# Two steps trade places in layer 3 of a four-layer transformer: keys and queries with a projection, a rotation with an addition

## The chip, the cores and the metric

The kernel runs on one core of one Trainium2 chip. The metric is the time of the whole program on the device in microseconds. The core's engines work side by side, each through its own list of instructions in order: TensorE (PE in the profile, its weight loads PEld), VectorE (DVE), ScalarE (ACT), GpSimd (POOL) and SyncE (SP), which issues transfers alone. GpSimd can issue transfers too, out of the same list as its arithmetic. The transfers of both run on the core's 16 DMA engines.

## What is computed

The input x has 4 batches of 1024 rows of 256 numbers, all in fp32. Four layers follow each other, each with a residual:

```python
x = x + attn_a(layernorm(x))     # layer 1: 16 heads of 64, no rotation
x = x + ffn(layernorm(x))        # layer 2: 256 -> 1024, gelu, -> 256
x = x + attn_b(layernorm(x))     # layer 3
x = x + ffn(layernorm(x))        # layer 4, the same weights as layer 2
```

Layer 3 normalises once more inside and adds that first normalised x as its residual. Its keys and queries come out of a narrow middle and are rotated by position:

```python
h = layernorm(x) * ln_scale + ln_bias
c_q, c_kv = h @ w_down_q.T, h @ w_down_kv.T            # 256 -> 128 each
q, k, v = (c @ up.T per head for the three w_up)       # 16 heads of 64
q, k = rope(q), rope(k)      # rows e, o -> e cos - o sin, e sin + o cos
out = softmax(q k^T / 8) v,  heads side by side,  @ w_out.T + x
```

## The kernel before

**Tiling.** A core's memory has 128 partitions, so two heads of 64 are worked on together, a *pair of heads*; there are 4 x 8 = 32 of them in an attention layer. For each, the 1024 queries are taken in 8 *steps* of 128. One step makes two score tiles of 128 x 1024 (`scores`, L238), their negated maxima on DVE (L249) and exponentials on ScalarE (L251), and one transposition in blocks of 32 on DVE (`turn`, L271, tile T). The blocks are then in the wrong partitions, and transfers bring them into the tile pT: of 15 for every two steps SyncE issues ten and GpSimd five (`send`, L295); in layer 3 one more is copied by ScalarE (`keep`, L287). Four to five steps later `weigh` (L304) multiplies pT by the values, `take` copies the sums (ScalarE, L314) and GpSimd divides them by the softmax's total (L316, tile oT, reading the totals out of pT). T and pT have two buffers each. The score tiles have three PSUM buffers, everything else that TensorE makes shares two (`group`).

**Projection.** `project` (L318 to L328) multiplies oT by the pair's rows of the output weights (L167 with `wo,oT`), ScalarE copies the product out of PSUM (`got`, L326), and GpSimd adds it to x (L328).

**Keys and queries.** While the steps of one pair of heads run, those of the next are made, in four turns, for two halves of the keys and two of the queries. `qk` multiplies (L167 with `hc,w`, four instructions) and copies to SBUF with a scale (L647). One step later `change` has GpSimd issue two transfers which bring each row to its neighbour's place (`turned`, L652, one buffer). One step after that `rotate` has GpSimd multiply by the cosines (L657, in place, so it too waits until the transfers have read the rows), multiply the turned rows by the sines (L658), and add (L659). `values` makes the values (L176, copied by L668) in two of the four turns.

**What sets the order.** The order is written out by hand in `steps_with` (L330 to L361): each engine does its part in the order in which the calls stand there. Odd jobs are put into `pieces` under the number of their step; a number lower by EARLY (0.5) puts them between the step's two halves of exponentials, a whole number at its end. With s the step:

- Even s: the scores of s+1; the five sends of GpSimd; `project`; the first exponentials of s+1; the pieces of s - 0.5, with `qk` and `values`; the second exponentials; the transposition of s; the pieces of s, with `rotate`.
- Odd s: the scores of s+1; the first exponentials; `weigh`; the second exponentials; `take`; the transposition; `keep`; the ten sends of SyncE; the pieces of s, with `change`.

The weights of a pair of heads are loaded by SyncE out of the same list as its sends (L636 and L212 to L214).

Of the kernel before, what the change touches and what calls it, by code (L numbers as in the profile page):

```python
# [9 lines left out]
F32 = mybir.dt.float32  # L10
# [5 lines left out]
P = 128  # L16
B, S, D = 4, 1024, 256
# [10 lines left out]
HB = 2  # L28
# [5 lines left out]
NK2 = S // DH  # L34
EPS = 1e-5
EARLY = 0.5


@with_exitstack
def hybrid_block_kernel(  # L40
# [5 lines left out]
    nc = tc.nc  # L46
# [18 lines left out]
    pp, tp, ptp, otp, tmp = pool("p", 2), pool("T", 2), pool("pT", 2), pool("oT", 1), pool("tmp", 1)  # L65
# [112 lines left out]
                    start=(i == 0), stop=(i == len(parts) - 1),  # L178
                )

    def attention(prep_batch, prep_pair, wo, loader, lead, kept):

# [18 lines left out]
        steps = [(g, qs) for g in range(len(pairs)) for qs in range(NT)]  # L203
        n = len(steps)
# [39 lines left out]
        def exponentials(s, j):  # L244
            if j == 0:
                probs[s] = pp.tile([P, NK, NG, SQ], F32, tag="p", name="p")
                total[s] = small.tile([P, 2], F32, tag="total", name="total")
            nmax = small.tile([P, 1], F32, tag="nmax", name="nmax")
            nc.vector.tensor_reduce(nmax, sc[s, j], AX.X, ALU.max, negate=True)  # L249
            place = j ^ (s % HB)  # L250
            nc.scalar.activation(  # L251
                probs[s][:, :NK2, ts(j, 2), :],
                sc.pop((s, j)).rearrange("p (k c i) -> p k c i", c=2, i=SQ), AF.Exp,
                bias=nmax, accum_out=total[s][:, place : place + 1],
            )
# [62 lines left out]
        def project(h):  # L318
            g, t0 = divmod(HB * h, NT)
            b, pr = pairs[g]  # L320
            po = group(HB, D)
            for t in range(HB):
                paired(po[:, t, :], [(oT[h][:, t], [wos[g][:, t]] * 2)])
            oT.pop(h)
            got = tmp.tile([P, HB, D], F32, tag="tmp", name="got")
            nc.scalar.copy(got, po)  # L326
            xd = xs[b][:, t0 : t0 + HB, :]
            nc.gpsimd.tensor_add(xd, xd, got)  # L328

        def steps_with(others):  # L330
            for k, f in others:
                pieces.setdefault(k, []).append(f)
            for s in range(-1, n + LAG + 1):
                h, part = divmod(s - LAG, HB)
                ahead = 0 <= s + 1 < n
                if 0 <= s < n:
                    invert(s)
                if ahead:
                    scores(s + 1)
                if part == 1 and 0 <= s // HB - 1 < n // HB:  # L340
                    send(s // HB - 1, nc.gpsimd, sent[len(sent) - POOL_DMA :])
                if part == 1 and 0 <= h < n // HB:
                    project(h)
                if ahead:
                    exponentials(s + 1, 0)
                for f in pieces.get(s - EARLY, ()):
                    f()
                if part == 0 and 0 <= h < n // HB:
                    weigh(h)
                if ahead:  # L350
                    exponentials(s + 1, 1)
                if part == 0 and 0 <= h < n // HB:
                    take(h)
                if 0 <= s < n:
                    turn(s)
                if part == 0 and 0 <= s // HB - 1 < n // HB:
                    keep(s // HB - 1)
                    T.pop(s // HB - 1)
                if part == 0 and 0 <= s < n:
                    send(s // HB, nc.sync, sent[: len(sent) - POOL_DMA])  # L360
                for f in pieces.get(s, ()):  # L361
                    f()

        return first, steps_with

# [126 lines left out]
    def layer_a():  # L492

        scale_a = 1.0 / (DH * DH * H)
        hTs = {}
        rows = Rows("a", (blocks[:1], blocks[1:2], blocks[2:]))

        def batch_a(b):
            work = []
            for qb in range(NQB):  # L500
                k = {}

                def straight(t, b=b, k=k, qb=qb):
                    if t == 0:
                        k["xn"] = xnp.tile([P, TQ, D], F32, tag="xn", name="xn")
                    dst, src = k["xn"][:, t, :], xs[b][:, qb * TQ + t, :]
                    shift, rstd = rows.factors(NQB * b + qb, t)[:2]
                    if b == 0 and qb == 1:
                        nc.vector.tensor_scalar(dst, src, rstd, shift, op0=ALU.mult, op1=ALU.add)
                    else:  # L510
                        standardize(dst, src, shift, rstd)

                def turned(c, b=b, k=k, qb=qb):
                    if c == 0:
                        p, tag = ((lowp, "low"), (highp, f"high{b % 2}"))[qb]
                        hTs[b, qb] = p.tile([P, NC, QB], F32, tag=tag, name="hT")
                    transposed(hTs[b, qb], k["xn"], c)

                work += [(10 * qb + t, lambda t=t, f=straight: f(t)) for t in range(TQ)]
                work += [(10 * qb + 6 + 2 * c, lambda c=c, f=turned: f(c)) for c in range(NC)]  # L520
            return work

        def pair_a(b, pr):
            made = {}

            def load():
                w = made["w"] = wp.tile([P, 3, NC, P], F32, tag="w", name="w")
                for i in (1, 0, 2):
                    nc.gpsimd.dma_start(
                        w[:, i], wqkv_a[i, :, ts(pr, P)].rearrange("(c p) f -> p c f", p=P)  # L530
                    )

            def qk(i, qb):
                name = ("qT", "kT")[i]
                if qb == 0:
                    made[name] = qkp.tile([P, S], F32, tag=name, name=name)
                pq = group(QB)
                paired(pq, [
                    (made["w"][:, i, c, :], [hTs[b, qb][:, c, :]] * 2) for c in range(NC)
                ])  # L540
                dst = made[name][:, ts(qb, QB)]
                if i == 0:
                    nc.scalar.mul(dst, pq, scale_a)
                else:
                    nc.scalar.copy(dst, pq)

            def values(m):
                if m == 0:
                    made["v"] = vp.tile([P, NK2, DH], F32, tag="v", name="v")
                pv = group(4, DH)  # L550
                for t in range(4):
                    qb, tt = divmod(4 * m + t, QB // DH)
                    by_head(pv[:, t, :], [
                        (hTs[b, qb][:, c, ts(tt, DH)], made["w"][:, 2, c, :]) for c in range(NC)
                    ])
                nc.scalar.copy(made["v"][:, ts(m, 4), :], pv)

            work = [(4 - 4 * i + 2 * qb - EARLY, lambda i=i, qb=qb: qk(i, qb)) for i in (1, 0) for qb in range(NQB)]
            work += [(6 + 2 * m, lambda m=m: values(m)) for m in range(NT // 2)]
            return {name: lambda name=name: made[name] for name in ("qT", "kT", "v")}, load, work  # L560


        later = [(4 + i, lambda i=i: rows.measure(2 + i // TQ, i % TQ)) for i in range(6 * TQ)]
        later += [(4 + 6 * TQ, lambda: rows.finish[2]())]
        first, steps = attention(batch_a, pair_a, wo_a, nc.gpsimd, lead=3, kept=0)
        loads, xn, pair = first[:2], first[2:14], first[14:]

        def measured(qb):
            for t in range(TQ):
                rows.measure(qb, t)  # L570
            rows.finish[qb]()

        def ready():

            nc.scalar.activation(small.tile([P, 1], F32, tag="nmax", name="ready"), eps, AF.Exp)


        first = loads + [lambda: measured(0)] + xn[:4] + [lambda: measured(1), ready] + xn[4:6] + pair[:1]
        first += xn[6:] + pair[1:3]
        later += [((-1, 0, 0, 1, 1)[i], f) for i, f in enumerate(pair[3:])]  # L580
        return first, lambda others: steps(later + others)


    def layer_b(rows):
# [45 lines left out]
        def pair_b(b, pr):  # L630
# [40 lines left out]
            for i in (1, 0):  # L671
                for qb in range(NQB):
                    k = 2 - 4 * i + 2 * qb
                    work += [(k - EARLY, lambda i=i, qb=qb: qk(i, qb))]
                    work += [(k + 1, lambda i=i, qb=qb: change(i, qb))]
                    work += [(k + 2, lambda i=i, qb=qb: rotate(i, qb))]
            work += [(4 + 2 * qb - EARLY, lambda qb=qb: values(qb)) for qb in range(NQB)]
            return {name: lambda name=name: made[name] for name in ("qT", "kT", "v")}, load, work

        return attention(batch_b, pair_b, wo_b, nc.sync, lead=5, kept=1)  # L680


    n_steps = B * NF * NT
# [72 lines left out]
```

## Time and profile before

| what | us |
|---|---|
| median of 3 runs | 3288.75 (3285.65 to 3289.74) |
| the profiled execution | 3283.29 |
| its span, first to last instruction | 3281.4 |
| layer 3's steps | about 1700 to 3060 of the span |
| busy over the span: PE, DVE, ACT, POOL | 3201.6, 2531.3, 2109.0, 1958.4 |

A row of the timeline has the start within the span, the duration, the engine, the line in the kernel, the instruction, what it writes and reads, shapes, and how many alike were merged; in brackets stands the time for which the engine was idle before it, and what ended that. A busy PE is not a PE at its peak, as the ends of matmuls are modelled. A row of the waits has the engine and line that waited, what it waited for, the total, the number of times and the longest. A wait for several things is put down to the one that came last by the profile, which can be wrong. DMA engines are no engine of the page's first line; their mean busy share is given for windows.

### The profile page before, as it was taken

How to read it: one execution, taken by the hardware profiler on the slowest of the kernel's cores; microseconds unless marked ns; L12 is line 12 of the kernel's file. 1: busy time of each engine (PE TensorE's matmuls, PEld its weight loads, DVE VectorE, ACT ScalarE, POOL GpSimd, SP SyncE). 2: the span in 40 equal slices, each digit the busy share in tenths (PEclk: the TensorE clock that was granted, in tenths of full speed). 3: DMA queues.
4: the chain of work that ended last, by engine and by line, in shares of the span. 5: the costliest groups of instructions: out<-in, count | busy, mean ns of one | idle time of the engine just before them, and what ended most of it. 6: DMA issues, size and time to landing. Idle time of an engine off the chain costs nothing.

```text
span 3281.4 us, 126564 instructions
## 1 busy us (share of the span) xinstructions
PE 3201.6 (98%) x52736; PEld 2022.3 (62%) x52736; DVE 2531.3 (77%) x2386; ACT 2109.0 (64%) x4304; POOL 1958.4 (60%) x2738
## 2 busy tenths in 40 slices
PE   8999999999999999999999999999999999998999
PEld 4666666666666666666555556666656666665666
DVE  7988888888888888941049889998989999998100
ACT  5666666666666666642447777777778777777332
POOL 4544454545444445430159888998989999996110
PEclk9999999999999999999999999999999999999999
DMA  8888888888888888840029889998888899998100
GB/s 226 224 220 213 226 223 222 219 227 223 222 214 218 222 229 225 218 116 0 2 81 237 223 217 240 242 240 236 240 229 240 240 243 247 245 246 214 38 20 20
DMA packets 244697, 642.13 MB, mean 196 GB/s; under 512 B 74304, under 2 KB 102976, under 8 KB 244128
## 3 DMA queue, kind: packets, MB, share of 16 engines
q1 hardware_dynamic: 161104, 397.60, 47.6%
q0 software_dynamic: 83024, 236.44, 25.8%
q8 instruction: 419, 6.86, 0.9%
q14 instruction: 150, 1.23, 0.1%
HBM read 43.39 MB, written 4.19 MB: 15 GB/s over the span
## 4 chain that ended last, share of the span: by engine, by line
PE 78%; SPq 8%; DMA 5%; DVE 3%; ACT 3%; issue 3%; POOL 1%; DVEq 0%; POOLq 0%; ACTq 0%
PE sc L238 23%; PE mm L304 21%; PE mm L167 16%; SPq L295 7%; PE mm L421 7%; PE ph L410 7%; PE mm L176 5%; DMA pT<-T 4%; DVE T L271 1%; DVE nmax L249 1%; ACT p L251 1%; PE mm L153 1%; POOL oT L316 0%; ACT gT L414 0%; SPq L214 0%
## 5 line engine op out<-in xcount | busy, mean ns | idle before, releaser
L249 DVE TENSOR_REDUCE nmax<-sc 128x1 f32<-128x1024 f32 x1024 | 1204.5, 1218 | 226.7 <-PE sc L238 223.5
L251 ACT ACTIVATE p<-sc,nmax 128x1024 f32<-128x1024 f32 x1024 | 1145.3, 1119 | 324.0 <-DVE nmax L249 324.0
L271 DVE STREAM_TRANSPOSE T<-p 128x2176 f32<-128x2176 f32 x512 | 1247.1, 2436 | 41.0 <-DMA pT<-T 17.6
L238 PE MATMUL sc<-kT,qT 64*64 64x512 f32 x8192 | 1085.5, 599 | 16.0 <-ACT p L251 10.6
L304 PEld LDWEIGHTS mm<-pT,v 64*64 64x64 f32 x32768 | 950.3, 133 | 145.6 <-issue 103.4
L304 PE MATMUL mm<-pT,v 64*64 64x128 f32 x32768 | 984.5, 269 | 14.5 <-issue 13.5
L295 POOL DMA_DIRECT2D pT<-T x1280 | 629.6, 499 | 121.1 <-PE sc L238 56.2
L316 POOL TENSOR_TENSOR oT<-oT,pT 128x256 f32<-128x256 f32 x256 | 186.1, 727 | 718.7 <-ACT oT L314 636.3
L238 PEld LDWEIGHTS sc<-kT,qT 64*64 64x64 f32 x8192 | 333.1, 133 | 409.9 <-issue 277.1
L328 POOL TENSOR_TENSOR x<-x,got 128x512 f32<-128x512 f32 x256 | 330.9, 1293 | 27.8 <-ACT got L326 23.9
L326 ACT COPY got<-mm 128x512 f32<-128x512 f32 x256 | 150.0, 586 | 283.0 <-PE mm L167 282.9
L428 DVE TENSOR_TENSOR x<-x,mm 128x512 f32<-128x512 f32 x32 | 22.0, 687 | 367.2 <-PE mm L421 367.1
L167 PE MATMUL mm<-wo,oT 128*64 128x256 f32 x2048 | 278.4, 393 | 19.6 <-POOL oT L316 18.6
L167 PEld LDWEIGHTS mm<-wo,oT 128*64 128x64 f32 x2048 | 124.6, 136 | 266.4 <-POOL oT L316 217.4
L414 ACT ACTIVATE gT<-ph,b_sb 128x512 f32<-128x512 f32 x128 | 87.5, 686 | 301.9 <-PE ph L410 301.8
L260 ACT COPY p<-total 128x128 f32<-128x128 f32 x512 | 151.8, 296 | 195.4 <-DVE total L259 188.5
L167 PE MATMUL mm<-hT,w 128*64 128x512 f32 x1024 | 242.9, 596 | 1.0 <-ACT hT L156 1.0
L421 PE MATMUL mm<-w_sb,gT 128*128 128x256 f32 x1024 | 226.0, 381 | 6.6 <-ACT hT L156 6.6
L410 PE MATMUL ph<-hT,w_sb 128*128 128x512 f32 x512 | 230.2, 603 | 0.5 <-ACT hT L156 0.5
L421 PEld LDWEIGHTS mm<-w_sb,gT 128*128 128x128 f32 x1024 | 193.1, 190 | 39.4 <-ACT hT L156 9.4
L396 POOL TENSOR_TENSOR x<-x,b_sb 128x256 f32<-128x256 f32 x64 | 44.5, 728 | 275.6 <-ACT xn L147 275.6
L251 ACT ACTIVATION_READ_ACCUMULATOR p<-sc,nmax 128x1 f32 x1024 | 205.3, 200 | 0.0
(90 smaller groups left out, 2473.1 us busy)
## 6 DMA issues: line engine op xcount, KB each, us to landing
pT<-T SPq DMA_DIRECT2D x2688, 136.0 KB, 4.7
pT<-T POOLq DMA_DIRECT2D x1280, 136.0 KB, 4.7
turned<-kT POOLq DMA_DIRECT2D x128, 128.0 KB, 3.5
turned<-qT POOLq DMA_DIRECT2D x128, 128.0 KB, 3.3
w<-in_wqkv_a POOLq DMA_DIRECT2D x96, 128.0 KB, 6.1
wo<-in_wo_a POOLq DMA_DIRECT2D x32, 128.0 KB, 5.4
wo<-in_wo_a POOLq DMA_DIRECT2D x64, 64.0 KB, 5.5
wo<-in_wo_b SPq DMA_DIRECT2D x32, 128.0 KB, 3.6
```

The source lines that it names most:

```text
L167: nc.tensor.matmul(out[ts(j, DH)], lhsT[:, ts(j, DH)], rhs[j], start=(first and i == 0), stop=(last and i == len(parts) - 1),)
L176: nc.tensor.matmul(out[ts(j, DH)], lhsT, rhs[:, ts(j, DH)], start=(i == 0), stop=(i == len(parts) - 1),)
L238: nc.tensor.matmul(sc[s, j][ts(half, DH), ts(m, 512)], qT()[rows, ts(2 * qs + half, DH)], kT()[rows, ts(m, 512)], start=True, stop=True,)
L249: nc.vector.tensor_reduce(nmax, sc[s, j], AX.X, ALU.max, negate=True)
L251: nc.scalar.activation(probs[s][:, :NK2, ts(j, 2), :], sc.pop((s, j)).rearrange("p (k c i) -> p k c i", c=2, i=SQ), AF.Exp, bias=nmax, acc ...
L271: nc.vector.transpose(T[h][:, :, q, :, :].rearrange("p c k i -> p k c i"), probs.pop(s))
L295: engine.dma_start(pT[h][ts(c, SQ), a], T[h][ts(a, SQ), c])
L304: nc.tensor.matmul(av[h][q][ts(j ^ q, DH)], v[ts(j, DH), k, :], pT[h][ts(j, DH), :, q, k, :], start=(k == 0), stop=(k == NK2 - 1),)
L316: nc.gpsimd.tensor_mul(parts, parts, pT.pop(h)[:, :, :, NK2, :])
L328: nc.gpsimd.tensor_add(xd, xd, got)
L410: nc.tensor.matmul(ph, w1_sb[:, c, ts(f, P)], hT[n][:, c, :], start=(c == 0), stop=(c == NC - 1),)
L421: nc.tensor.matmul(po[n][:, t % 2, :], gT[n][:, f, ts(t, P)], w2_sb[:, f, :], start=(f == 0), stop=(f == NF - 1),)
```

## The change

In layer 3 alone, `qk` moves from the place of EARLY to a new, earlier one (FIRST, 0.75), which lies directly ahead of `project`. `project` no longer copies and adds; it returns `fetch`, which copies and returns the addition. With `late` the copy comes after the first exponentials, and the addition at the very end of the step, after `rotate`. Layer 1 is called with `late=False`, which keeps its order. `values` stays where it is. No instruction is added or taken away.

```diff
+FIRST = 0.75
...
         for t in range(HB):
             paired(po[:, t, :], [(oT[h][:, t], [wos[g][:, t]] * 2)])
         oT.pop(h)
-        got = tmp.tile([P, HB, D], F32, tag="tmp", name="got")
-        nc.scalar.copy(got, po)
+
+        def fetch():
+            got = tmp.tile([P, HB, D], F32, tag="tmp", name="got")
+            nc.scalar.copy(got, po)
+            return lambda: nc.gpsimd.tensor_add(xd, xd, got)
+
         xd = xs[b][:, t0 : t0 + HB, :]
-        nc.gpsimd.tensor_add(xd, xd, got)
+        return fetch
...
-                if part == 1 and 0 <= h < n // HB:
-                    project(h)
+                for f in pieces.get(s - FIRST, ()):
+                    f()
+                fetch = project(h) if part == 1 and 0 <= h < n // HB else None
+                if fetch and not late:
+                    fetch()()
                 if ahead:
                     exponentials(s + 1, 0)
+                add = fetch() if fetch and late else None
                 for f in pieces.get(s - EARLY, ()):
                     f()
...
                 for f in pieces.get(s, ()):
                     f()
+                if add:
+                    add()
...
-                    work += [(k - EARLY, lambda i=i, qb=qb: qk(i, qb))]
+                    work += [(k - FIRST, lambda i=i, qb=qb: qk(i, qb))]
```

More of the change, by code (lines that the diff above doesn't have):

```diff
@@ L179, in by_head, with attention @@
                 )
-    def attention(prep_batch, prep_pair, wo, loader, lead, kept):
+    def attention(prep_batch, prep_pair, wo, loader, lead, kept, late):
         pairs = [(b, pr) for b in range(B) for pr in range(NF)]
@@ L564, in layer_a @@
         later += [(4 + 6 * TQ, lambda: rows.finish[2]())]
-        first, steps = attention(batch_a, pair_a, wo_a, nc.gpsimd, lead=3, kept=0)
+        first, steps = attention(batch_a, pair_a, wo_a, nc.gpsimd, lead=3, kept=0, late=False)
         loads, xn, pair = first[:2], first[2:14], first[14:]
@@ L678, in pair_b @@
             return {name: lambda name=name: made[name] for name in ("qT", "kT", "v")}, load, work
-        return attention(batch_b, pair_b, wo_b, nc.sync, lead=5, kept=1)
+        return attention(batch_b, pair_b, wo_b, nc.sync, lead=5, kept=1, late=True)
     n_steps = B * NF * NT
```

## The prediction

> **What bounds the kernel now.** I read the page first, then the windows, then one pair of steps in the timeline, then the waits. The page's first part, and windows over nearly all of layer 3 and over eight of its pairs of steps:
>
> ```profile
> PE 3201.6 (98%) x52736; PEld 2022.3 (62%) x52736; DVE 2531.3 (77%) x2386; ACT 2109.0 (64%) x4304; POOL 1958.4 (60%) x2738
> ```
>
> ```profile
> 1800.00:3000.00 1200.00, 1167.19 (x21732) 738.69 (x21728) 1093.82 (x943) 919.48 (x1841) 1068.62 (x1387) 1.00 0.89 237
> 2654.00:2734.00 80.00, 80.00 (x1508) 50.67 (x1504) 75.80 (x65) 61.81 (x124) 74.25 (x96) 1.00 0.94 248
> ```
>
> After the sum the columns are PE, PEld, DVE, ACT and POOL busy, the granted clock, the DMA engines' share, GB/s. GpSimd's 60% over the span is 93% in the eight pairs (74.25 of 80), DVE 95%, the DMA engines 94%. No engine has a microsecond to give in ten. One pair, first its even step:
>
> ```profile
> 2411.87 0.73 POOL L316 TENSOR_TENSOR oT<-oT,pT 128x256 f32<-128x256 f32 x1
> 2412.55 1.14 POOL L652 DMA_DIRECT2D turned<-kT  x2
> 2412.78 1.08 PE L167 MATMUL mm<-wo,oT 128*64 128x256 f32 x8
> 2413.68 2.44 POOL L295 DMA_DIRECT2D pT<-T  x5
> 2413.69 1.03 PE L167 MATMUL mm<-hc,w 128*64 128x512 f32 x4
> 2413.96 0.59 ACT L326 COPY got<-mm 128x512 f32<-128x512 f32 x1 [0.66 <-PE mm L167]
> 2414.45 1.12 ACT L251 ACTIVATE p<-sc,nmax 128x1024 f32<-128x1024 f32 x1
> 2415.55 0.60 ACT L647 ACTIVATE kT<-mm 128x512 f32<-128x512 f32 x1
> 2415.71 0.21 PEld L238 LDWEIGHTS sc<-kT,qT 64*64 64x64 f32 x8 [0.87 <-ACT p L251]
> 2416.14 1.30 POOL L328 TENSOR_TENSOR x<-x,got 128x512 f32<-128x512 f32 x1
> 2417.38 1.28 POOL L657 TENSOR_TENSOR kT<-kT,cos_sb 128x512 f32<-128x512 f32 x1
> 2421.75 0.73 POOL L316 TENSOR_TENSOR oT<-oT,pT 128x256 f32<-128x256 f32 x1 [0.50 <-DMA pT<-T]
> ```
>
> The loop that sets an undisturbed pair's 10.01 us is to be seen here: the projection (L167 from oT) follows the scores, the copy `got` follows it, the first exponential follows `got`, and the next scores wait 0.87 for that exponential, which frees their PSUM. GpSimd runs beside it: one multiplication (L316), two transfers of the turned rows (L652), five sends (L295), the addition (L328), three operations of the rotation, and 0.50 of waiting.
>
> **The change, by parts.** (1) *Keys or queries ahead of the projection.* Four matmuls of 1.03 move ahead of eight of 1.08, and the copy of 0.60 (L647) takes the place of `got` (0.59) ahead of the first exponential. Where L316 is in time the exponential starts where it did: between 0.05 earlier and 0.01 later; I take 0. Where L316 is late, something is won:
>
> ```profile
> PE mm L167 <- POOL oT L316: 17.4, 22, 3.3
> SPq L295 <- POOL oT L316: 17.3, 15, 3.5
> POOL qT L657 <- DMA turned<-qT: 8.3, 10, 1.4
> POOL kT L657 <- DMA turned<-kT: 7.8, 11, 1.1
> ```
>
> (waits between 1800 and 3000; total us, times, longest.) Counting from the end of the scores, the projection stood 19.9 us in 29 of the 114 pairs that lie whole between 1790 and 2990. Keys fill at most 0.93 of each (1.03 less the overlap of two groups), so 13.9. Layer 3 has 124 such pairs (32 pairs of heads by four turns, less the first four), so times 124/114: **-15.1 us**.
>
> (2) *`got` after the first exponential.* It trades places with L647, at equal length, and stands before the second exponential. It costs nothing while the projection ends before the first exponential does, 1.6 us later than now. Without that cover DVE, which in the same timeline works 9.84 of the 10.01 (four maxima 4.72, two transpositions 4.88, two reciprocals 0.24), would be late by the excess over 0.17. Nothing else on ScalarE queues behind it, and its reader, the addition, now comes 4 us later anyway.
>
> (3) *The rotation ahead of the addition.* No work is added. But L657 must wait for the two L652 transfers, and the addition of 1.29 was what stood between the last send and L657. From issue to landing (the turned tile's own view):
>
> ```profile
> DMA to landing us min/median/max: 2.0/3.4/5.3
> ```
>
> The second transfer is issued 0.57 after the first, the five sends end 1.14 + 2.43 = 3.57 after the first, so at the median the later transfer lands 0.57 + 3.4 - 3.57 = 0.4 after the sends, at the longest 2.3. Taken pair by pair from the landings, the wait without the addition is 0.74 on average (quarters at 0.12, 0.63, 1.06), against 0.16 that is waited now: 0.59 more in each pair. The Trainium skill speaks against this order in DMA: Bandwidth & Descriptors, Rules for kernel authors: issue early, compute, and wait late. Its price, in Anatomy of one DMA (fixed 2.0 us plus the bytes at 436 GB/s), would give an estimated 2.3 for these 128 KB, which lands 0.7 before the sends end: no wait at all, and only part (1) left, -15. The row says 3.4, on engines that are 94% busy, and the row decides.
>
> What takes the 0.59: GpSimd idles 0.72 a pair before L316 now, more than enough on average, but in 57 of 114 pairs less than what is added. Without waits its cycle is 9.33 (9.73 in its fastest pairs, less 0.40 of waiting); with 0.74 it is 10.07, above the loop's 10.01. So lateness of L316 builds up over undisturbed stretches and is worked off in disturbed ones (the mean pair is 10.52).
>
> What is late next: L316, behind it the transfers and sends of its own queue, the projection, and SyncE's sends, which wait until L316 has read the old pT (the second line of the waits). The projection tolerates 0.93 of keys plus the 0.29 by which L316 now ends ahead of the scores: 1.2, and up to 0.6 more in pairs without values, where PE stands before the scores anyway. SyncE tolerates on average 1.45: 0.43 in which it is still issuing weights, and 1.02 between the last landing and the transposition that reuses the tile two pairs on; a quarter of the pairs tolerate under 0.77. I carried the lateness through the 114 pairs, each with its own landing and idle time, and let the loop lose what exceeds a tolerance: 43.7 us lost at a tolerance of zero, 30.4 at 0.6, 24.0 at 1.0, 20.0 at 1.5. I take 1.0 to 1.5, times 124/114: 21.8 to 26.2, **+24 us**.
>
> GpSimd's sends to pT are late too, by a microsecond or so; they land about 3 us before SyncE's last one, so they cost nothing; were that cover gone, the transposition would wait. kT and qT are ready earlier, and nobody waits for them. The weights of the earlier matmuls land some 10 us ahead of their first use. Layer 1 has the old order.
>
> **Sum.** -15 + 0 + 24 = +9. The profiled execution took 3283.3 (span 3281.4 and 1.9 around it), so 3292 for its like; the runs' median lies 5.5 higher, at 3288.75, so **3298 us**.
>
> **Rivals.** *Faster:* the transfers land sooner than now, since the queue they share with SyncE's sends stands otherwise, or the idle time before L316 swallows the wait. With waits half as long the same carrying gives -11.5 at tolerance 1.0, with none -13.9: -13 to -15 for the layer, 3275. It decides from an average wait below 0.6, where loss and gain are even. For it: idle exceeds added wait on average. Against: 57 pairs in which it doesn't. *No change:* gain and loss even out, 3289; for it speaks that `got` and the keys' copy are of one length, so the loop keeps its 10.01 either way. *Much slower:* SyncE has no tolerance. Its sends start with L316 late, the DMA engines stand idle and then lag, the transposition waits. That is the tolerance of zero: 43.7 x 1.09 - 15.1 = +33, 3321; for it speak the engines' 94%, and a longer landing works alike (waits 20% longer at tolerance 1.0: +26). Against: most pairs have SyncE's last landing 0.6 or more ahead.
>
> **How the numbers follow.** Runs of this kernel can tell about 0.2%, 6.6 us. Chances: slower by 9 (7 to 12) 0.40, faster 0.24, no change 0.20, much slower 0.16. The first case reaches down to the 6.6 bound; I leave it with slower, as landings under load rather grow. Faster 0.24, same 0.20, slower 0.56. The range goes from 3272, a little below the case without waits (a loop 0.05 shorter in the 57 pairs without values adds 3), to 3325, just above the case without tolerance. The likeliest case's own range is 3289 to 3310.
>
> **What would show it.** (1) right: no wait of PE L167 on L316 above a few us, `got` behind the exponential in the timeline. (2) right: the second exponential not waiting for `got`. (3) right: L657's waits for the turned transfers grow from 16 to some 85 us, L328 directly ahead of L316, the 0.72 before L316 nearly gone, SyncE's waits for L316 above 17. If L657 waits under 60 us in total, the faster rival has won; if DVE's transposition waits tens of us for its transfers, the much slower one. Wrong altogether would be a shift in the undisturbed pair's 10.01, which no step of mine moves.

## The result and the profile after

The changed kernel takes 3300.34 us in the median of 15 runs, the kernel before 3285.78 in 15; the ratio is 1.0039, with a 95% interval of 1.003 to 1.0049. That is 12.8 us of 3286 (the prediction said 9); the two medians lie 14.6 apart. The profiled execution took 3299.06, its span is 3297.2.

The same two windows over layer 3, with the sum and then PE, PEld, DVE, ACT and POOL busy, the clock, the DMA engines' share and GB/s:

```profile
1800.00:3000.00 1200.00, 1150.85 (x21392) 710.41 (x21381) 1077.38 (x931) 911.40 (x1818) 1052.26 (x1370) 0.99 0.88 234
2654.00:2734.00 80.00, 80.00 (x1506) 49.10 (x1502) 74.98 (x64) 61.34 (x124) 70.92 (x93) 1.00 0.92 244
```

In the same 1200 us every engine gets less done: DVE begins 931 instructions instead of 943. In the eight pairs GpSimd falls from 74.25 busy to 70.92, not for want of work. Rows from the timeline of two pairs after the change, others left out, show why (L317 is now the multiplication into oT, L663 the turned rows' transfers, L296 the sends, L668 the rotation's first operation, L329 `got`, L330 the addition):

```profile
2652.37 0.73 POOL L317 TENSOR_TENSOR oT<-oT,pT 128x256 f32<-128x256 f32 x1 [0.56 <-ACT oT L315]
2653.04 1.13 POOL L663 DMA_DIRECT2D turned<-qT  x2
2653.41 1.08 PE L168 MATMUL mm<-hc,w 128*64 128x512 f32 x4
2654.17 2.43 POOL L296 DMA_DIRECT2D pT<-T  x5
2654.32 1.03 PE L168 MATMUL mm<-wo,oT 128*64 128x256 f32 x8
2654.54 0.60 ACT L658 ACTIVATE qT<-mm 128x512 f32<-128x512 f32 x1 [0.88 <-PE mm L168]
2655.03 1.11 ACT L252 ACTIVATE p<-sc,nmax 128x1024 f32<-128x1024 f32 x1
2656.12 0.58 ACT L329 COPY got<-mm 128x512 f32<-128x512 f32 x1
2657.12 1.27 POOL L668 TENSOR_TENSOR qT<-qT,cos_sb 128x512 f32<-128x512 f32 x1 [0.52 <-DMA turned<-qT]
2660.93 1.29 POOL L330 TENSOR_TENSOR x<-x,got 128x512 f32<-128x512 f32 x1
2662.40 0.73 POOL L317 TENSOR_TENSOR oT<-oT,pT 128x256 f32<-128x256 f32 x1 [0.19 <-ACT oT L315]
...
2668.07 1.28 POOL L668 TENSOR_TENSOR qT<-qT,cos_sb 128x512 f32<-128x512 f32 x1 [1.43 <-DMA turned<-qT]
...
2673.29 0.73 POOL L317 TENSOR_TENSOR oT<-oT,pT 128x256 f32<-128x256 f32 x1
```

The wait for the turned rows, 0.52 and then 1.43, stands where the addition stood, and the idle time ahead of L317 shrinks from 0.56 to 0.19 to nothing. Keys and queries run ahead of the projection, `got` behind the exponential, with no wait of its own here. The waits of layer 3 (total us, times, longest), after the change, between 1800 and 3000:

```profile
PE mm L168 <- POOL oT L317: 28.8, 34, 2.2
POOL kT L668 <- DMA turned<-kT: 51.7, 48, 2.7
POOL qT L668 <- DMA turned<-qT: 41.5, 43, 2.3
DVE T L272 <- DMA pT<-T: 24.4, 21, 3.1
SPq L296 <- POOL oT L317: 38.8, 37, 3.4
```

The same for the transposition before the change:

```profile
DVE T L271 <- DMA pT<-T: 7.9, 11, 2.0
```

The turned rows' landing after the change:

```profile
DMA to landing us min/median/max: 1.9/3.4/5.6
```

The transfers land as they did (3.4 in the median); what changed is that somebody stands waiting: 93.2 us instead of 16.1. The waits of TensorE and SyncE for L317 went up behind that. So did those of DVE's transposition: 60 us in all instead of 20, of which 42 instead of 13 are put down to transfers and the rest mostly to ScalarE.

One measure recurs below. *GpSimd's cycle* is the time from one of its multiplications into oT to the next, less the idle time just ahead of the latter, in pairs of steps in which GpSimd has no odd job besides the operations named so far, in the median. It was 9.36 before and is 10.14 after, against 10.01 for an undisturbed pair before the change.

### The profile page after: what moved, and what is told of

It is laid out like the page before. It is cut to its first block, busy times and chain, and to the rows that moved or that the text cites. A ratio compares the mean times of both kernels' runs of the same rounds, so it can differ in the third digit from the quotient of the medians.

```text
span 3297.2 us, 126564 instructions
## 1 busy us (share of the span) xinstructions
PE 3200.7 (97%) x52736; PEld 2004.9 (61%) x52736; DVE 2529.9 (77%) x2386; ACT 2111.2 (64%) x4304; POOL 1953.7 (59%) x2738
## 4 chain that ended last, share of the span: by engine, by line
PE 66%; SPq 15%; DMA 8%; DVE 3%; issue 3%; POOL 3%; ACT 2%; DVEq 0%; POOLq 0%; ACTq 0%
PE sc L239 18%; PE mm L305 17%; SPq L296 14%; PE mm L168 13%; DMA pT<-T 7%; PE mm L432 7%; PE ph L421 7%; PE mm L177 4%; DVE T L272 1%; DVE nmax L250 1%; POOL oT L317 1%; POOL x L330 1%; ACT p L252 1%; SPq L215 1%; PE mm L154 0%
## 5 line engine op out<-in xcount | busy, mean ns | idle before, releaser
L239 PE MATMUL sc<-kT,qT 64*64 64x512 f32 x8192 | 1072.4, 600 | 18.7 <-ACT p L252 12.3
L296 POOL DMA_DIRECT2D pT<-T x1280 | 629.7, 499 | 117.3 <-PE sc L239 56.9
L317 POOL TENSOR_TENSOR oT<-oT,pT 128x256 f32<-128x256 f32 x256 | 185.8, 726 | 660.2 <-ACT oT L315 648.2
L239 PEld LDWEIGHTS sc<-kT,qT 64*64 64x64 f32 x8192 | 317.7, 133 | 379.8 <-issue 290.6
L330 POOL TENSOR_TENSOR x<-x,got 128x512 f32<-128x512 f32 x256 | 329.0, 1285 | 20.4 <-ACT got L329 18.4
L329 ACT COPY got<-mm 128x512 f32<-128x512 f32 x256 | 149.7, 585 | 171.2 <-PE mm L168 170.7
```

The source lines that it names most:

```text
L239: nc.tensor.matmul(sc[s, j][ts(half, DH), ts(m, 512)], qT()[rows, ts(2 * qs + half, DH)], kT()[rows, ts(m, 512)], start=True, stop=True,)
L296: engine.dma_start(pT[h][ts(c, SQ), a], T[h][ts(a, SQ), c])
L317: nc.gpsimd.tensor_mul(parts, parts, pT.pop(h)[:, :, :, NK2, :])
L330: return lambda: nc.gpsimd.tensor_add(xd, xd, got)
```

## The experiments

Each time is a median, each ratio is to the kernel before on the same chip, for which 3282.2 to 3285.8 were measured. A single execution can lie some 10 us off its kernel's median (the profiled one of the first experiment took 3284.3), so verdicts are taken from the ratios, and places from the traces.

**Keys ahead without the rotation ahead.**

```diff
+                if add:
+                    add()
                 for f in pieces.get(s, ()):
                     f()
-                if add:
-                    add()
```

> The changed kernel with the addition to x back ahead of the rotation; keys and queries stay ahead of the projection and the copy 'got' stays behind the first exponentials. Theory A (the rotation's new place is what costs, keys ahead of the projection gain): L657's successor waits for the turned transfers for about 17 us in layer 3 again, TensorE's wait for L316's successor stays small, time 3286 - 15 = 3271, ratio to before 0.9954, not above 0.998. Rival B (the keys ahead or the late 'got' cost): same or slower than before, 3286 to 3300.

Measured: 3276.28, ratio 0.9972 (0.9965 to 0.998), so 9.2 us faster. Its waits:

```profile
PE mm L168 <- POOL oT L317: 9.8, 8, 3.4
POOL kT L668 <- DMA turned<-kT: 9.2, 13, 1.5
POOL qT L668 <- DMA turned<-qT: 4.8, 6, 1.7
```

The first half of the change is a gain, smaller than the 15 expected; TensorE's wait for the multiplication went down from 17.4. The profiled execution is one of this kernel's slower ones, no faster than the one profiled before the change, so its waits show the places better than the sizes. The distance from here to the changed kernel is the price of the rotation's place: 1.0039 less 0.9972, 22 us (by the intervals, some 4 either way). This kernel beats both the one before and the changed one.

**The rotation ahead alone.**

```diff
                 fetch = project(h) if part == 1 and 0 <= h < n // HB else None
-                if fetch and not late:
-                    fetch()()
+                add = fetch() if fetch else None
+                if add and not late:
+                    add()
+                    add = None
...
-                add = fetch() if fetch and late else None
...
-                    work += [(k - FIRST, lambda i=i, qb=qb: qk(i, qb))]
+                    work += [(k - EARLY, lambda i=i, qb=qb: qk(i, qb))]
```

> The rotation ahead of the addition alone: keys and queries back behind the projection, 'got' copied directly after it, as before. Theory A: the lateness of GpSimd now meets a projection that has no keys in front of it and stands ahead of the first exponential, with 0.3 us of tolerance; carried through the pairs this loses 36 x 1.09 = 39 us: 3325, ratio 1.012, clearly slower than the changed kernel (1.0039). Rival B: as before or at most as the changed kernel, 3286 to 3300.

Measured: 3310.62, ratio 1.0076 (1.0064 to 1.0088): 25 us slower than before, and clearly slower than the changed kernel.

```profile
PE mm L168 <- POOL oT L317: 38.7, 42, 2.2
POOL kT L669 <- DMA turned<-kT: 54.5, 50, 2.9
POOL qT L669 <- DMA turned<-qT: 34.3, 37, 2.2
```

89 us of waiting for the turned rows, nearly as in the changed kernel, without keys ahead. So the loss belongs to the rotation. But 39 had been expected for a tolerance of 0.3, and the loss is 25 here against 22 with keys in front, the same within the intervals: the tolerance matters far less than the prediction's carrying of lateness from pair to pair had it.

**Where `got` stands.** As the first experiment, with the copy directly behind the projection:

```diff
                 fetch = project(h) if part == 1 and 0 <= h < n // HB else None
-                if fetch and not late:
-                    fetch()()
+                add = fetch() if fetch else None
+                if add and not late:
+                    add()
+                    add = None
                 if ahead:
                     exponentials(s + 1, 0)
-                add = fetch() if fetch and late else None
```

> As e1_keys, but 'got' is copied directly after the projection, ahead of the first exponential, so that both copies stand ahead of it. My account of the loop (projection or keys, copy, first exponential, scores of the next step): each undisturbed pair grows from 10.01 by some 0.55, 124 x 0.55 = 68 us over e1_keys: about 3340, ratio 1.016. Rival (TensorE, VectorE or the DMA engines set the pair's 10.01 and ScalarE's order does not matter): within 10 us of e1_keys.

Measured: 3346.02, ratio 1.0181 (1.0168 to 1.0194), 69.7 over the first experiment, where 68 were expected. The timeline of ScalarE:

```profile
2660.06 0.60 ACT L659 ACTIVATE kT<-mm 128x512 f32<-128x512 f32 x1 [0.88 <-PE mm L168]
2660.98 0.58 ACT L329 COPY got<-mm 128x512 f32<-128x512 f32 x1 [0.32 <-PE mm L168]
2661.46 1.12 ACT L252 ACTIVATE p<-sc,nmax 128x1024 f32<-128x1024 f32 x1
```

The first exponential stands behind both copies and the end of the projection. The loop runs where the prediction put it: the order on ScalarE alone, with no work added, lengthens every undisturbed pair. The agreement of the sums is partly luck: undisturbed pairs went from 9.95 to 10.87, by 0.92 and not 0.55 (0.32 of waiting comes on top of the copy), but disturbed pairs hide much of it, and the mean pair grew from 10.50 to 11.02.

**The rotation a pair of steps later**, to take the landing away without moving the addition:

```diff
-    lowp, highp, xnp, rp = pool("low", 2), pool("high", 1), pool("xn", 1), pool("rope", 1)
+    lowp, highp, xnp, rp = pool("low", 2), pool("high", 1), pool("xn", 1), pool("rope", 2)
...
-                    work += [(k + 2, lambda i=i, qb=qb: rotate(i, qb))]
+                    work += [(k + 4, lambda i=i, qb=qb: rotate(i, qb))]
...
-    b2_sb = const.tile([P, D], F32, name="b2_sb")
+    b2_sb = w2_sb[:, 0, :]
...
-        nc.gpsimd.dma_start(b2_sb, b2.partition_broadcast(P))
```

> The changed kernel, but each rotation comes one pair of steps later, with two buffers for the turned rows, so that the transfers have some 10 us more to land; to make room b2 is not loaded and a row of w2 is added in its place. Theory A: the rotation's waits for turned vanish (below 5 us), what part (1) gains is left: 3271 or a little less, ratio 0.995. Rival (it is the addition's place behind the rotation, not the landing, that costs): stays at 3300, ratio 1.004.

Measured: 3456.18, ratio 1.0518. A miss by another cause, as the waits show:

```profile
PE sc L238 <- POOL qT L669: 128.6, 27, 6.6
```

(Between 1800 and 3100.) The waits for the turned rows are gone, but a pair of steps later is too late for the first half of the queries. Its rotation (under step 6 of the pair before, where it was 4) now stands at the end of the last even step before the next pair of heads starts, and GpSimd finishes it some 4 us after TensorE could have made that pair's first scores, which read it:

```profile
2014.81 1.26 POOL L669 TENSOR_TENSOR qT<-qT,turned 128x512 f32<-128x512 f32 x1
2016.12 3.57 PE L238 MATMUL sc<-kT,qT 64*64 64x512 f32 x16 [4.26 <-POOL qT L669]
```

In the trace it is the first of the pair's two query rotations that ends these waits, each time, once for nearly every pair of heads. The kernel also leaves out b2 and adds a row of w2 in its place. The run tells nothing on the question it was made for.

**The transfers sooner.** The turned rows' transfers are issued at the end of the even step, behind the previous rotation; once with the addition first (from the first experiment), once with the changed kernel's order.

```diff
-                    work += [(k + 1, lambda i=i, qb=qb: change(i, qb))]
+                    work += [(k, lambda i=i, qb=qb: change(i, qb))]
```

> As e1_keys, but the transfers of the turned rows are issued half a step to a step sooner, at the end of the even step behind the previous rotation, instead of behind GpSimd's multiplication in the odd step. They then have some 4 us more to land, no buffer is added and every rotation stays in its step. Theory A: the rotation's waits (14 us in e1_keys) vanish, 3272 to 3276, ratio 0.996. If the gain of e1_keys is limited by the transposition's waits for transfers (46 us there against 20 before), nothing more is won: 3276.

> The changed kernel with the turned rows' transfers issued sooner as in e5_keys_sooner; the addition stays behind the rotation. Theory A (what costs is that the landing is exposed): the rotation's waits fall from 101 us to under 10 and the whole loss is gone: 3276, ratio 0.997, as e1_keys. Rival (the place of the addition itself costs, or the late 'got'): 3300, ratio 1.004.

Measured: 3292.21, ratio 1.0024 (1.0016 to 1.0032) with the addition first, and 3289.11, ratio 1.0018 (1.001 to 1.0025) in the changed kernel's order. In the second, half of the loss is gone; in the first, all of the gain. The landing of the turned rows is waited for no more in either (below 0.5 us in layer 3; the 101 us in the expectation are over the whole layer). GpSimd's timeline in the first of the two shows what came in its place:

```profile
2664.11 0.74 POOL L317 TENSOR_TENSOR oT<-oT,pT 128x256 f32<-128x256 f32 x1
2665.14 2.48 POOL L296 DMA_DIRECT2D pT<-T  x5 [0.29 <-POOL oT L317]
2667.64 1.29 POOL L330 TENSOR_TENSOR x<-x,got 128x512 f32<-128x512 f32 x1
2668.87 1.27 POOL L668 TENSOR_TENSOR kT<-kT,cos_sb 128x512 f32<-128x512 f32 x1
2670.10 1.28 POOL L669 TENSOR_TENSOR turned<-turned,sin_sb 128x512 f32<-128x512 f32 x1
2671.45 1.29 POOL L670 TENSOR_TENSOR kT<-kT,turned 128x512 f32<-128x512 f32 x1
2673.03 1.13 POOL L663 DMA_DIRECT2D turned<-kT  x2 [0.29 <-POOL kT L670]
2674.19 0.74 POOL L317 TENSOR_TENSOR oT<-oT,pT 128x256 f32<-128x256 f32 x1
```

A transfer that GpSimd issues directly behind its own arithmetic, and that must wait for that arithmetic, starts 0.29 late, where its operations otherwise follow each other with an overlap of 0.06. It happens twice in each pair: the sends need the pT that L317 has just read, the transfers the `turned` that L670 has just read. Twice 0.35 makes a cycle of 10.06 and 10.13 out of 9.36, as long as with the waits. So neither run had taken away what the theory says costs; they had exchanged it. That the first of them loses 17 us to the first experiment, with no landing in sight, speaks for the cycle. It does not show that the cycle alone costs, for SyncE's waits for the multiplication rose as well, from 21.6 us in the first experiment to 65.8 here, and were 55.3 in the second of the two:

```profile
SPq L296 <- POOL oT L317: 65.8, 61, 5.1
```

**SyncE freed from the multiplication**, to see whether the loss runs through its sends. The kernel then leaves out the division by the softmax's totals in layer 3:

```diff
-            nc.gpsimd.tensor_mul(parts, parts, pT.pop(h)[:, :, :, NK2, :])
+            by = pT.pop(h)[:, :, :, NK2, :]
+            if kept:
+                by = cos_sb[:, : HB * P].rearrange("p (a q i) -> p a q i", a=NG, q=HB)
+            nc.gpsimd.tensor_mul(parts, parts, by)
```

> The changed kernel, in which layer 3's multiplication L317 takes its factor from the cosine table instead of pT (the division by the softmax's totals is left out there). SyncE's sends then no longer wait for that multiplication. If most of the loss runs through SyncE and the transposition: the time falls by 10 us or more beyond what the same does for the kernel before, to about 3287. If it runs through the projection and GpSimd's own queue: it falls by what e8_before_free falls and at most 4 us more, 3293 to 3300.

> The kernel before, with layer 3's factor from the cosine table instead of pT (the division is left out there), for comparison with e7_free. SyncE waited 17 us for the multiplication in the trace of before, and the transposition 20 us for transfers: 3286 to 3276, ratio 0.997 to 1.0.

Measured: 3305.04, ratio 1.0062 (1.0045 to 1.0079) for the changed kernel, 3285.6, ratio 1.0011 (1.0 to 1.0021) for the kernel before. SyncE's waits for the multiplication are gone and the transposition's waits fall from 60 to 36 us (those for transfers from 42 to 30), and still nothing is won; TensorE's wait is larger:

```profile
PE mm L168 <- POOL oT L320: 38.6, 45, 2.4
```

As long as the landing stays exposed, the loss does not need SyncE's waits for the multiplication. GpSimd's cycle is 10.19 here.

**Freed, and the transfers sooner**: the changed kernel freed as above (so again without the division), with the transfers at the end of the even step behind the addition (LAST is a key between a step's end and the next one's start). No transfer then follows the arithmetic that it needs, and the landing should be covered, while addition and `got` keep their late places:

```diff
+LAST = 0.125
...
                 if add:
                     add()
+                for f in pieces.get(s + LAST, ()):
+                    f()
...
-                    work += [(k + 1, lambda i=i, qb=qb: change(i, qb))]
+                    work += [(k + LAST, lambda i=i, qb=qb: change(i, qb))]
```

> e7_free (the changed kernel, layer 3's factor from the cosine table, so the division is left out there), with the turned rows' transfers issued sooner, at the end of the even step behind the addition. No transfer of GpSimd then waits for the arithmetic just before it, which is what filled the cycle in e5_keys_sooner and e6_sooner (0.35 us twice in a pair). Theory A (GpSimd's cycle is what costs): the cycle falls from 10.19 to about 9.4, the idle time ahead of the multiplication is back above 0.5, TensorE's wait for it falls under 12 us, time 3276, ratio 0.997. Rival (the late place of the addition or of 'got' costs): as e7_free, ratio 1.005.

Measured: 3258.03, ratio 0.9929 (0.9915 to 0.9942): by the ratios 23 us faster than before, and 44 faster than the same kernel with the transfers in their old place.

```profile
PE mm L169 <- POOL oT L321: 14.1, 12, 3.8
POOL qT L674 <- DMA turned<-qT: 6.2, 10, 1.4
POOL kT L674 <- DMA turned<-kT: 4.3, 9, 1.0
```

So with the landing covered, the late addition and the late `got` do not bring the loss. Three of the expected signs came out otherwise: TensorE's wait is 14.1, not under 12; the idle time ahead of the multiplication is 0.24; and the cycle reads 9.92, since the sends themselves now stand (0.32 a pair), while GpSimd's busy time in a pair is 9.30. The gain is also larger than expected. GpSimd's cycle cannot be its whole cause: it was 9.48 in the first experiment, which is slower by the ratios (0.9972). The transposition's waits are down to 14 us, and how much of the gain is theirs was not separated. Not run were the first experiment freed in this way, and these transfers without the freeing.

**A sixth send on GpSimd** in layer 3, for the changed kernel, for the first experiment and for the kernel before:

```diff
+        mine = POOL_DMA + kept
...
-                    send(s // HB - 1, nc.gpsimd, sent[len(sent) - POOL_DMA :])
+                    send(s // HB - 1, nc.gpsimd, sent[len(sent) - mine :])
...
-                    send(s // HB, nc.sync, sent[: len(sent) - POOL_DMA])
+                    send(s // HB, nc.sync, sent[: len(sent) - mine])
```

> The changed kernel with six sends of layer 3 on GpSimd and nine on SyncE instead of five and ten. Theory A: the sixth send of 0.49 falls into the wait for the turned rows, so the wait shrinks by about as much, the cycle stays near 10.15, and the time stays within 5 us of the changed kernel or falls a little as SyncE has less to do: 3290 to 3300. Rival (GpSimd's busy time is what counts, not the exposed landing): cycle 10.6, some 50 us more, 3345.

> e1_keys with six sends on GpSimd and nine on SyncE. If SyncE's transfers, which the transposition waits for (46 us in e1_keys), are what keeps e1_keys from the full 15 us: the transposition's waits fall under 25 us, GpSimd's cycle rises to 9.9 and stays under the pair's 10.01, time 3268 to 3274, ratio 0.995 to 0.997. If GpSimd's 9.9 is already too much: 3285 to 3295.

> The kernel before with six sends on GpSimd and nine on SyncE, for comparison with e10_six and e11_keys_six. Its projection has no keys ahead of it, so a GpSimd cycle of 9.85 is late more often: 3286 to 3296, ratio 1.0 to 1.004.

Measured: the changed kernel 3287.57, ratio 1.0018 (1.0009 to 1.0026); the first experiment 3273.67, ratio 0.9973 (0.9962 to 0.9983); the kernel before 3285.57, ratio 1.0007 (0.9999 to 1.0014). The changed kernel's waits with six sends:

```profile
POOL kT L670 <- DMA turned<-kT: 27.1, 39, 2.0
POOL qT L670 <- DMA turned<-qT: 16.8, 31, 1.9
```

GpSimd was given 0.49 more to do in each pair, and the changed kernel got 7 us faster (0.21%, a little more than expected), where the kernel before got no faster. The send fills half of the exposed wait (93 to 44 us), the cycle stays (10.04), and SyncE has one send less. Added to the first experiment, the send changes nothing: GpSimd's cycle rises from 9.48 to 9.82. The 46 us of the expectation are all waits of the transposition in the first experiment's trace, of which only 33 were put down to transfers; with the sixth send these are 37 and 23. So the waits for transfers fell by 10 us and the time did not follow. The thought that SyncE's transfers keep that kernel from its full gain is not borne out; what does is left open.

## Why the prediction was right

*The sum.* +9 was forecast, +12.8 measured. Its two terms, taken apart: -15.1 for the keys ahead, measured -9.2; +24 for the rotation ahead, measured +22 with keys ahead (the distance to the first experiment) and +25 without. That +24 came so close is in part luck: it was read off the carrying at tolerances of 1.0 to 1.5, and the same carrying at 0.3 gave 39 where 25 was measured.

*Part (1), keys ahead.* The sign is right, the size of this term was too large by 6. The step that gave it was "Keys fill at most 0.93 of each (1.03 less the overlap of two groups), so 13.9". TensorE's wait fell from 17.4 to 9.8, not to near nothing; why is open. And a part of what was won came from where 0 had been put: an undisturbed pair takes 9.95 with keys ahead and 10.01 without, in every trace with `got` in its place of before or behind the exponential. The bound of 0.05 earlier had been stated; the value taken should have been that end. The prediction also called a shift of the 10.01 a sign that it was wrong altogether; it shifted, by 0.06, and nothing else hung on it.

*Part (2), `got` behind the exponential.* Right: no cost of it shows there, and directly behind the projection it costs 70 us. One reading ahead of it was wrong without harm: that no engine had a microsecond to give in ten. ScalarE, busy for 61.81 of 80 us, had more than two.

*Part (3), the rotation ahead.* Right in place and size. The wait for the turned rows was to grow "from 16 to some 85 us"; it is 93. GpSimd's cycle was put at 10.07 and is 10.14 in the median. The idle time ahead of the multiplication went from 0.80 to 0.29 in pairs without extra work. The Trainium skill's price for a transfer (DMA: Bandwidth & Descriptors, Anatomy of one DMA) would have given no wait; the row of the trace, 3.4, held after the change too.

*What is late next.* Here the account was too fine. TensorE was to wait for the multiplication no more than a few us: it waits 28.8, more than before. The tolerances were to decide between 20 and 44 us of loss; taking the keys' 0.93 away (the second experiment) changed the loss from 22 to 25. And the sign that was to tell the much slower rival, tens of us of waiting for transfers at the transposition, came without it: those waits are 42 us after the change, but they rose to 33 in the first experiment too, which is faster, and freeing SyncE from the multiplication won nothing back. In the second experiment, which lost 25 us, they were only 8 us. So the loss does not need the transposition's waits.

*The rivals.* Faster needed waits under 0.6 on average; they are 0.83. What it counted on, idle time that exceeds the added wait on average, was there and did not help. That lateness builds up over several pairs, as the prediction had it, fits this, but no run shows it by itself.

## What to carry to other kernels

In this loop a transfer's landing was free only while the issuing engine had work between issue and wait, so before two steps trade places, look which of them stood in that gap. An engine's average idle time does not show that it can take a wait: with a cycle of 9.4 us in a loop of 10.0, a wait that rose to 0.83 on average and scattered up to 2.7 made the loop slower. If the gap can't be kept, put other work of that queue into it (here one more send won back 7 us), and check that no transfer then comes directly behind the arithmetic that it depends on.

## What the runs showed of the hardware

A transfer issued by GpSimd that waits for GpSimd's own operation just ahead of it starts 0.29 us after that operation's end; without such a wait the issue starts 0.06 before the end that the trace gives. Two of these in each pair made GpSimd's cycle as long as the exposed landing did (10.06 and 10.13 against 10.14), though the time fell by half of the loss in the changed kernel's order. With the transfers behind the addition and the sends freed from the multiplication, the same order was 29 us faster still (0.9929 against 1.0018). That was not foreseen.
